# A third shared block between attention and experts, with all row scatters issued there

## The chip, the cores and the metric

The kernel runs on one core of a Trainium2 chip. The metric is device microseconds of one execution; each version is run several times and the median is given. A profiled execution leaves a page and a trace, from which the readings come. The engines are PE (TensorE matmul; PEld is its weight load), DVE (VectorE), ACT (ScalarE), POOL (GpSimd) and SP (SyncE, used for DMA issue).

## The reference

One transformer layer on x of 4 x 1024 tokens with D = 256, all in float32.

```
x = x + xattn(layernorm(x), ctx)      # 16 heads, 77 context rows, own norm with gamma, beta
x = x + ffn(layernorm(x))

ffn:  scores = softmax(xf @ Wg); weights, indices = top_k(scores, 4)      # 32 experts
      for e in experts:  y[tok] += swiglu(xf[tok], W1[e], W2[e], W3[e]) * w
      return y + swiglu(xf, Ws1, Ws2, Ws3)                                # the shared expert
swiglu(x, w1, w2, w3) = (silu(x @ w1) * (x @ w3)) @ w2
```

## The kernel before

The 4096 tokens are eight blocks of 512 (`NB`), each of four tiles of 128. The program has four stages, and in each the order of instructions on every engine is the order of the program text (`as_written`).

**Attention loop** (t = 0 to 31, L756 to L830). One tile of 128 tokens per turn, with the routing of older blocks woven in: `turn_ffn` transposes a block's normalized tokens and stores them to DRAM (`xnd`), `gate`, `chances`, `choose`, `mark`, `count` and `place` find each token's four experts and the row it takes in the expert's list. `send` then scatters rows: one indirect DMA from POOL (L674) writes 128 rows of 272 floats to `xr` in DRAM. A block has 16 of them. The loop issues four a turn from t = 11 on, which leaves the last 12 of block 5 and all of blocks 6 (`y`) and 7 (`z`).

**Between loop and experts** (L833 to L1004). The list `left` holds row scatters not yet issued, and `sends(n)` issues the next n. The routing of blocks y and z is finished here, the tables of which expert tile reads which rows are made (`tables`, a generator advanced by `next`; table "a" serves the first 64 tiles, "z" the rest), and the shared expert is computed for blocks y and z. The shared expert of a block comes in parts: `shared_in(blk, f, act)` does eight PE passes of 512 columns (L704) and the activation on ACT (L713), `shared_mid(blk, f)` multiplies on DVE into hT (L719, or L721 and L722 for block y), `shared_out(blk)` does 16 PE passes (L730) and `shared_add(blk)` two DVE additions onto the result y0 (L743). In this stage hT has one buffer and sg two; PSUM has eight banks, all under one tag.

**Experts** (L1126 to L1183). 144 tiles of 128 rows. Per tile: two transposes (L1078), copy on DVE (L1080), four matmul passes (L1086), Silu on ACT (L1094) and a product on DVE (L1095), a transpose (L1100) with copy on ACT (L1102), the second matmul (L1107), scaling on DVE (L1111), and one indirect DMA from POOL that scatters the 128 result rows to `ys` (L1112), from one of six y buffers. The steps of four tiles are interleaved. SP fetches the rows of eight tiles at a time (L1024), each with its own DMA, into one of two buffers g. Fetches for the first 64 tiles wait for the scatters of blocks 0 to 5; later ones wait for all. Every third tile up to j = 45 issues one left row scatter as well (`sends(1)`). The last 16 tiles or so stand under a `Switch` on the number of tiles; shared block 0 is computed around its entry.

**End** (L1227 to L1254). The shared blocks 1 to 5, and for each half block a load of its tokens' four results from `ys` (`gather`, 1 MB, on SP), three DVE additions (`gathered`, L1204 to L1206) and a store to `out`. `adding` says which half blocks are added during which shared block; `order` begins with blocks 6 and 7.

The names of tiles in the profile: xr rows by expert, ys results by token, ph and hT the shared hidden layer, pz its output, peh an expert's hidden layer, h its activation, xnd and sx the stored tokens for the shared expert.

Of the kernel before, what the change touches and what calls it, by code (L numbers as in the profile page):

```python
# [9 lines left out]
F32 = mybir.dt.float32  # L10
I32 = mybir.dt.int32
U32 = mybir.dt.uint32
AF = mybir.ActivationFunctionType
# [17 lines left out]
def kernel(  # L31
# [723 lines left out]
    with as_written():  # L755
        for t in range(NT):  # L756
            blk, c = t // NC, t % NC
            ffn, old = blk - 1, blk - 2
            ahead = blk + 1 < NB
            if c == 0 and blk + 2 < NB:  # L760
                xts[blk + 2] = load(blk + 2)
            if t == 0:

                nc.sync.dma_start(xr[NE * PLACES :, :], none)
                nc.sync.dma_start(
                    xr[: NE * PLACES, :].rearrange("(e q) r -> q e r", q=PLACES)[:P],
                    none.unsqueeze(1).to_broadcast([P, NE, ROW]),
                )
            if t == 18:
                nc.sync.dma_start(ws13[:, :, 0, :], Ws1.rearrange("(k p) f -> p k f", p=P))  # L770
                nc.sync.dma_start(ws13[:, :, 1, :], Ws3.rearrange("(k p) f -> p k f", p=P))
                nc.sync.dma_start(ws2, Ws2.rearrange("(k p) f -> p k f", p=P))
            if t in parts:
                load_experts(*parts[t])
            if c == 1 and ahead:
                scale_in(blk + 1)
            if c == 1 and ffn >= 0:
                measure_out(ffn, 2, 4)
            if c == 3 and ahead:
                bias_in(blk + 1)  # L780
            if c == 3:
                measure_out(blk, 0, 2)
            if c == 3 and ffn >= 0:
                measure_ffn(ffn)
            if c == 1 and old >= 0:
                gate(old)
            if c == 3 and old >= 0:
                count(old)
            sv = [scores(t, g) for g in range(2)]
            if c == 1 and old >= 0:  # L790
                turn_gate(old)
                chances(old)
            soften(t, 0, sv[0])
            if c == 1 and old >= 0:
                powers(old)
            soften(t, 1, sv[1])
            sv.append(scores(t, 2))
            if t >= 1:
                for i in range(3):
                    turn_p(t - 1, i)  # L800
            soften(t, 2, sv[2])
            if c == 0 and old >= 0:
                turn_ffn(old)
            if c == 2 and ahead:
                turn_in(blk + 1)
            if c == 0 and ahead:
                measure_in(blk + 1)
            if c == 1 and old >= 0:
                choose(old)
            if c == 2 and old >= 0:  # L810
                mark(old)
            if c == 3 and old >= 0:
                place(old)
            invert(t)
            divide(t)
            if c == 1 and ahead:
                norm_in(blk + 1)
            if c == 3 and ffn >= 0:
                norm_ffn(ffn)
            if c == 3:  # L820
                settle(blk, 0)
            elif ffn >= 0:
                settle(ffn, c + 1)
            if c >= 2 and ahead:
                keep(blk + 1, 2 * c - 4, 2 * c - 2)
            if t >= 11:
                b11, c11 = divmod(t - 11, NC)
                send(b11, c11 * TOPK, (c11 + 1) * TOPK)
            if t >= 1:
                residual(t - 1, output(t - 1))  # L830


        z, y = NB - 1, NB - 2  # L833
        assert BA == y
        msum_a = sm.tile([P, NE], F32, tag="msum_a", name="msum_a", bufs=1)
        nc.vector.tensor_copy(msum_a, cums[BA][:, 0, :])
        left = [(y - 1, i) for i in range(NK)]

        def sends(n):
            for blk, i in left[:n]:  # L840
                send(blk, i, i + 1)
            del left[:n]

        del left[:4]
        measure_out(z, 2, 3)
        settle(z, 1)
        sends(3)
        turn_ffn(y)
        for i in range(3):
            turn_p(NT - 1, i)  # L850
        settle(z, 2)
        residual(NT - 1, output(NT - 1))
        measure_out(z, 3, 4)
        gate(y)
        turn_gate(y)
        chances(y)
        powers(y)
        settle(z, 3)
        sends(2)
        measure_ffn(z)  # L860
# [94 lines left out]
    with as_written():  # L955
        for part in range(5):
            load_experts(*parts[NT + 1 + part])
        ta = tables("a", msum_a, NA)
        choose(y)
        shared_in(y, 0, AF.Tanh)  # L960
        norm_ffn(z)
        mark(y)
        sends(7)
        shared_mid(y, 0)
        next(ta)
        shared_in(y, 1, AF.Tanh)
        turn_ffn(z)
        count(y)
        gate(z)
        next(ta)  # L970
        place(y)
        assert not left
        left += [(y, i) for i in range(NK)]
        turn_gate(z)
        chances(z)
        powers(z)
        next(ta)
        shared_mid(y, 1)
        shared_out(y)
        next(ta)  # L980
        choose(z)
        shared_in(z, 0, AF.Silu)
        mark(z)
        count(z)
        msum_z = sm.tile([P, NE], F32, tag="msum_z", name="msum_z", bufs=1)
        nc.vector.tensor_copy(msum_z, cums[NB][:, 0, :])
        tz = tables("z", msum_z, NJ - NA)
        sends(5)
        shared_mid(z, 0)
        place(z)  # L990
        left += [(z, i) for i in range(NK)]
        shared_in(z, 1, AF.Silu)
        shared_add(y)
        shared_mid(z, 1)
        sends(11)
        shared_out(z)
        shared_add(z)
    late_stack.close()
# [126 lines left out]
    with as_written():  # L1125
        fetch(0)  # L1126
        for j in range(NM_ + len(steps)):
            if j % RG == 1 and j + RG - 1 <= NM_:
                fetch(j + RG - 1)
            if j in (4 * RG + 4, 5 * RG + 4, 6 * RG + 4):  # L1130
                fetch_shared(j // RG - 4, nc.sync)
            for i, step in enumerate(steps):
                jj = j - i
                if 0 <= jj < NM_:
                    made[jj, i + 1] = step(jj, made.pop((jj, i), None))
            if j % 3 == 0:
                sends(1)
            if j in (2, 5, 8, 11):
                next(tz)
            if j < NM_ and j % RG in (0, 1, 2):  # L1140
                find(j // RG * RG, j % RG)
            if j == NM_ - 2 * RG:
                more = {
                    e: nc.values_load(
                        tabs["more"],
                        engines=[e],
                        min_val=0,
                        max_val=(NJ - NM_) // RG,
                        skip_runtime_bounds_check_because="at most as many tiles as are laid out",
                    )  # L1150
                    for e in mybir.ALL_ENGINES
                }
                tc.switch_hint(more, (NJ - NM_) // RG + 1, label="more")

            if j == NM_:
                shared_in(0, 0, AF.Silu)
            if j == NM_ + 1:
                shared_mid(0, 0)
                shared_in(0, 1, AF.Silu)
            if j == NM_ + 2:  # L1160
                shared_mid(0, 1)
                fetch_shared(3, nc.scalar)
    ahead = groups[NM_ // RG][0]
    for n in tc.Switch(more, (NJ - NM_) // RG + 1, hint="more"):
        end = NM_ + n * RG
# [3 lines left out]
        with as_written():  # L1169
            for j in range(NM_, end + len(steps)):  # L1170
# [6 lines left out]
                if j < end and j % RG in (0, 1, 2):  # L1177
                    find(j // RG * RG, j % RG)
                if j == end:
                    shared_out(0)  # L1180
                if j == end + 1:
                    shared_add(0)
    bp_stack.close()  # L1183
    hs_stack.close()
    bw_stack.close()
# [31 lines left out]

    NS = NB - 2
    order = [*range(2 * NS, 2 * NB), *range(2 * NS)]
    adding = [[], [0, 1, 2, 3], [4, 5, 6], [7, 8, 9], [10, 11, 12], [13, 14, 15]]  # L1220
    with as_written():
        come = [gather(hb) for hb in order[:8]]

# [2 lines left out]
            if i + 8 < 2 * NB:  # L1226
                come.append(gather(order[i + 8]))  # L1227

        shared_in(1, 0, AF.Silu)
        shared_in(1, 1, AF.Silu)  # L1230
        shared_mid(1, 0)
        for blk in range(1, NS):
            todo = list(adding[blk])
            last = blk == NS - 1
            if blk + 3 < NS:
                fetch_shared(blk + 3, nc.scalar)
            for i in todo[:1]:
                add(i)
            shared_mid(blk, 1)
            for i in adding[blk - 1]:  # L1240
                store(order[i])
            if last:
                store(order[todo[0]])
            if not last:
                shared_in(blk + 1, 0, AF.Silu)
            shared_out(blk)
            for i in todo[1:2]:
                add(i)
            if not last:
                shared_mid(blk + 1, 0)  # L1250
                shared_in(blk + 1, 1, AF.Silu)
            for i in todo[2:]:
                add(i)
            shared_add(blk, store if last else None)  # L1254

# [54 lines left out]
```

## Time and profile before

| | us |
|---|---|
| median of 3 runs (798.32 to 802.23) | 800.97 |
| the profiled execution | 800.8 |
| its span, first to last instruction | 799.0 |
| PE busy in the span | 733.9 (92%) |
| DVE | 527.1 (66%) |
| POOL | 402.9 (50%) |
| ACT | 334.1 (42%) |

| Stage, by the trace | us from the span's start |
|---|---|
| the last attention output (L497) ends | 401.2 |
| first expert product on PE (L1086) | 449.3 |
| last row scatter (L674) | 554.7 |
| last result scatter (L1112) | 732.2 |
| first gather issued (L1196) | 735.8 |
| last addition (L743) | 794.0 |

All times are read from one execution, counted from its first instruction. A row of the timeline gives start and length in us, engine, line, operation and tiles, and in brackets the idle time of that engine before it and what ended it. "issue" is a wait for nothing that the profile shows; "remote" one that something outside the shown instructions ended. The granted clock of TensorE is 1.00 at full speed; over the span it is 0.974.

### The profile page before, as it was taken

How to read it: one execution, taken by the hardware profiler on the slowest of the kernel's cores; microseconds unless marked ns; L12 is line 12 of the kernel's file. 1: busy time of each engine (PE TensorE's matmuls, PEld its weight loads, DVE VectorE, ACT ScalarE, POOL GpSimd, SP SyncE). 2: the span in 40 equal slices, each digit the busy share in tenths (PEclk: the TensorE clock that was granted, in tenths of full speed). 3: DMA queues.
4: the chain of work that ended last, by engine and by line, in shares of the span. 5: the costliest groups of instructions: out<-in, count | busy, mean ns of one | idle time of the engine just before them, and what ended most of it. 6: DMA issues, size and time to landing. Idle time of an engine off the chain costs nothing.

```text
span 799.0 us, 12911 instructions
## 1 busy us (share of the span) xinstructions
PE 733.9 (92%) x3508; PEld 542.2 (68%) x3508; DVE 527.1 (66%) x1455; ACT 334.1 (42%) x1586; POOL 402.9 (50%) x488
## 2 busy tenths in 40 slices
PE   6999999999999999999968578879999999999796
PEld 4775767777777777776735457667888878776454
DVE  1874565778777787767665355545767666473897
ACT  0647667676666677766521112221222222221000
POOL 2003333347777777777886355555555555443000
PEclk9999999999999999999998889999999999999988
DMA  8930000404135221513175244465555545422996
GB/s 269 333 101 1 1 1 1 132 1 141 58 100 185 80 98 57 162 57 115 57 242 169 75 125 136 138 197 165 189 165 162 182 146 160 149 96 90 412 412 246
DMA packets 78867, 111.97 MB, mean 140 GB/s; under 512 B 9995, under 2 KB 63679, under 8 KB 78783
## 3 DMA queue, kind: packets, MB, share of 16 engines
q1 hardware_dynamic: 59519, 66.14, 26.7%
q0 software_dynamic: 13056, 36.72, 12.7%
q10 hardware_dynamic: 6208, 8.17, 2.9%
q8 instruction: 31, 0.51, 0.3%
q14 instruction: 53, 0.43, 0.2%
HBM read 62.36 MB, written 48.64 MB: 139 GB/s over the span
## 4 chain that ended last, share of the span: by engine, by line
PE 72%; DVE 10%; ACT 6%; issue 4%; DMA 4%; POOL 3%; DVEq 0%; ACTq 0%; SPq 0%; POOLq 0%
PE peh L1086 16%; PE po L497 14%; PE sc L430 13%; PE py L1107 7%; ACT p L446 5%; PE pgT L1078 4%; PE ph L704 3%; PE pz L730 3%; PE pp L479 2%; PE phT L1100 2%; PE pvo L262 1%; POOL xr L674 1%; PE pvo L287 1%; PE pm L262 1%; DMA gy<-ys 1%
## 5 line engine op out<-in xcount | busy, mean ns | idle before, releaser
L1112 POOL DMA_INDIRECT ys<-y,place x144 | 138.0, 959 | 130.0 <-DVE y L1111 81.2
L446 ACT ACTIVATE p<-sc,mx 128x77 f32<-128x77 f32 x512 | 159.1, 350 | 93.2 <-DVE mx L438 93.2
L1086 PE MATMUL peh<-we,gT 128*128 x576 | 155.0, 393 | 17.7 <-issue 11.4
L497 PE MATMUL po<-we,pT 128*128 128x256 f32 (+1 forms) x640 | 147.1, 383 | 4.6 <-DVE pT L484 3.3
L674 POOL DMA_INDIRECT xr<-xn,row x128 | 127.6, 997 | 35.6 <-issue 34.6
L461 POOL TENSOR_TENSOR p<-p,su 128x385 f32<-128x385 f32 (+1 forms) x96 | 91.0, 973 | 97.2 <-DVE su L456 76.3
L430 PE MATMUL sc<-we,qT 128*128 128x385 f32 (+1 forms) x384 | 138.9, 509 | 0.9 <-POOL qT L416 0.9
L497 PEld LDWEIGHTS po<-we,pT 128*128 128x128 f32 (+1 forms) x640 | 118.4, 190 | 26.7 <-DVE pT L484 5.4
L1094 ACT ACTIVATE h<-peh 128x128 f32<-128x128 f32 x144 | 40.1, 278 | 217.2 <-PE peh L1086 143.8
L1086 PEld LDWEIGHTS peh<-we,gT 128*128 128x128 f32 x576 | 101.5, 196 | 29.7 <-issue 12.8
L446 ACT ACTIVATION_READ_ACCUMULATOR p<-sc,mx 128x1 f32 x512 | 118.7, 232 | 0.0
L430 PEld LDWEIGHTS sc<-we,qT 128*128 128x128 f32 x384 | 71.1, 189 | 54.3 <-issue 27.7
L1095 DVE TENSOR_TENSOR h<-peh,h 128x128 f32<-128x128 f32 x144 | 41.8, 291 | 84.6 <-ACT h L1094 69.1
L1107 PE MATMUL py<-we,ehT 128*128 x288 | 88.3, 389 | 0.9 <-ACT ehT L1102 0.8
L1111 DVE TENSOR_SCALAR y<-py,own 128x256 f32<-128x256 f32 x144 | 69.5, 483 | 17.2 <-PE py L1107 13.1
L438 DVE TENSOR_REDUCE mx<-sc 128x5 f32<-128x385 f32 (+1 forms) x96 | 54.3, 576 | 33.8 <-PE sc L430 31.3
L1080 DVE COPY gT<-pgT 128x256 f32<-128x256 f32 x144 | 59.8, 415 | 7.4 <-PE pgT L1078 4.8
L1078 PE MATMUL pgT<-ident,g 128*128 128x128 f32 x288 | 55.9, 278 | 1.1 <-issue 0.4
L1107 PEld LDWEIGHTS py<-we,ehT 128*128 128x128 f32 x288 | 44.5, 195 | 12.6 <-ACT ehT L1102 1.7
L1078 PEld LDWEIGHTS pgT<-ident,g 128*128 128x128 f32 x288 | 40.6, 144 | 16.9 <-issue 1.6
L1100 PE MATMUL phT<-ident,h 128*128 128x128 f32 x144 | 40.2, 279 | 8.2 <-DVE h L1095 5.9
L730 PE MATMUL pz<-ws,hT 128*128 128x256 f32 x128 | 35.5, 431 | 11.8 <-DVE hT L719 6.3
(200 smaller groups left out, 927.4 us busy)
## 6 DMA issues: line engine op xcount, KB each, us to landing
g<-xr SPq DMA_DIRECT2D x144, 136.0 KB
gy<-ys SPq DMA_DIRECT2D x16, 1024.0 KB
xr<-y SPq DMA_DIRECT2D x1, 4352.0 KB
y<-in_x SPq DMA_DIRECT2D x8, 512.0 KB
out<-y ACTq DMA_DIRECT2D x16, 256.0 KB
xnd<-xnT SPq DMA_DIRECT2D x6, 512.0 KB
we<-in_W SPq DMA_DIRECT2D x8, 384.0 KB
ys<-y,place POOLq DMA_INDIRECT x144
```

What stands on the lines that cost most here:

```text
L430: nc.tensor.matmul(sc[:, : (h1 - h0) * SK], qTs[blk][:, k, o : o + P], mq[:, b, k, h0 * SK : h1 * SK], start=(k == 0), stop=(k == KC - 1),)
L446: nc.scalar.activation(probs[t][:, h, :], sv[:, h - h0, :], AF.Exp, bias=mx[:, h : h + 1], accum_out=su[:, h : h + 1],)
L461: nc.gpsimd.tensor_tensor(p[:, h0:h1, :], p[:, h0:h1, :], su[:, h0:h1].unsqueeze(2).to_broadcast([P, h1 - h0, SK]), ALU.mult,)
L497: nc.tensor.matmul(po[:, :D], pT[:n, i, :], vo[b][:n, i, :], start=(i == 0), stop=(i == KT - 1))
L674: sct = nc.gpsimd.indirect_dma_start(out=xr, out_offset=bass.IndirectOffsetOnAxis(ap=row[:, i : i + 1], axis=0), in_=xn[:, c, :], in_offse ...
L730: nc.tensor.matmul(pz[:, c * D : (c + 1) * D], hT[:, f, (2 * c2 + c) * P : (2 * c2 + c + 1) * P], ws2[:, f, :], start=(f == 0), stop=(f == ...
L1078: nc.tensor.transpose(pt[:, k * P : (k + 1) * P], g[:, j % RG, k * P : (k + 1) * P], ident)
L1080: nc.vector.tensor_copy(gT.rearrange("p k t -> p (k t)"), pt[:, :D])
L1086: nc.tensor.matmul(ph[:, : 2 * H], gT[:, k, :], we[:, ds(ev[j] * EW + k * 2 * H, 2 * H)], start=(k == 0), stop=(k == KC - 1),)
L1107: nc.tensor.matmul(py[:, :D], hT, we[:, ds(ev[j] * EW + KC * 2 * H, D)], start=True, stop=True)
L1111: nc.vector.tensor_scalar(y, py[:, :D], own[:, i, 1:2], None, ALU.mult)
L1112: sent = nc.gpsimd.indirect_dma_start(out=ys, out_offset=bass.IndirectOffsetOnAxis(ap=place_[:, i : i + 1], axis=0), in_=y, in_offset=None,)
```

## The change

Block 0's shared expert moves from the switch into the stage between loop and experts. Its tokens are loaded from `xnd` into a buffer of the attention loop (tag qb), on SP. All row scatters of blocks y and z are issued in that stage, in two runs of 12 and 20, with `place(z)` between them; the expert loop issues none. `choose(z)` stands ahead of `shared_out(y)`. Block 1 takes block 0's place in the switch. The end computes the shared blocks 2 to 5, and the 16 half blocks are spread four to a block.

```
+        sxs[0] = late.tile([P, NC, D], F32, tag="qb", name="sx_0", bufs=3)
+        sxs[0] = sxs[0].rearrange("p c d -> p (c d)").rearrange("p (k t) -> p k t", k=KC)
+        nc.sync.dma_start(sxs[0], xnd[0])
         z, y = NB - 1, NB - 2
...
         next(ta)
         shared_mid(y, 1)
+        shared_in(0, 0, AF.Silu)
+        choose(z)
         shared_out(y)
         next(ta)
-        choose(z)
-        shared_in(z, 0, AF.Silu)
         mark(z)
+        shared_mid(0, 0)
+        shared_in(0, 1, AF.Silu)
         count(z)
...
         tz = tables("z", msum_z, NJ - NA)
-        sends(5)
-        shared_mid(z, 0)
+        sends(12)
         place(z)
         left += [(z, i) for i in range(NK)]
+        shared_mid(0, 1)
+        shared_in(z, 0, AF.Silu)
+        shared_add(y)
+        shared_out(0)
+        shared_mid(z, 0)
         shared_in(z, 1, AF.Silu)
-        shared_add(y)
+        shared_add(0)
         shared_mid(z, 1)
-        sends(11)
+        sends(20)
+        assert not left
         shared_out(z)
         shared_add(z)
...
             if j in (4 * RG + 4, 5 * RG + 4, 6 * RG + 4):
-                fetch_shared(j // RG - 4, nc.sync)
+                fetch_shared(j // RG - 3, nc.sync)
...
-            if j % 3 == 0:
-                sends(1)
...
             if j == NM_:
-                shared_in(0, 0, AF.Silu)
+                shared_in(1, 0, AF.Silu)
...
-                fetch_shared(3, nc.scalar)
+                fetch_shared(4, nc.scalar)
...
-    adding = [[], [0, 1, 2, 3], [4, 5, 6], [7, 8, 9], [10, 11, 12], [13, 14, 15]]
+    adding = [[], [], [0, 1, 2, 3], [4, 5, 6, 7], [8, 9, 10, 11], [12, 13, 14, 15]]
...
-        shared_in(1, 0, AF.Silu)
-        shared_in(1, 1, AF.Silu)
-        shared_mid(1, 0)
-        for blk in range(1, NS):
+        shared_in(2, 0, AF.Silu)
+        shared_in(2, 1, AF.Silu)
+        shared_mid(2, 0)
+        for blk in range(2, NS):
...
-            for i in todo[:1]:
+            for i in todo[: 1 + last]:
                 add(i)
             shared_mid(blk, 1)
             for i in adding[blk - 1]:
                 store(order[i])
             if last:
-                store(order[todo[0]])
+                for i in todo[:2]:
+                    store(order[i])
```

The rest of block 0's calls in the switch (`shared_mid`, `shared_out`, `shared_add`) change to block 1 in the same way.

More of the change, by code (lines that the diff above doesn't have):

```diff
@@ L1155 @@
             if j == NM_:
-                shared_in(0, 0, AF.Silu)
+                shared_in(1, 0, AF.Silu)
             if j == NM_ + 1:
-                shared_mid(0, 0)
-                shared_in(0, 1, AF.Silu)
+                shared_mid(1, 0)
+                shared_in(1, 1, AF.Silu)
             if j == NM_ + 2:
-                shared_mid(0, 1)
-                fetch_shared(3, nc.scalar)
+                shared_mid(1, 1)
+                fetch_shared(4, nc.scalar)
     ahead = groups[NM_ // RG][0]
@@ L1179 @@
                 if j == end:
-                    shared_out(0)
+                    shared_out(1)
                 if j == end + 1:
-                    shared_add(0)
+                    shared_add(1)
     bp_stack.close()
@@ L1246 @@
             shared_out(blk)
-            for i in todo[1:2]:
+            for i in todo[1 + last : 2 + last]:
                 add(i)
@@ L1251 @@
                 shared_in(blk + 1, 1, AF.Silu)
-            for i in todo[2:]:
+            for i in todo[2 + last :]:
                 add(i)
```

## The prediction

> **What bounds the kernel now.** I read the busy rows by slice first, then a table of stages, then the timelines of POOL and ACT inside the worst stage, and last the chain of waits.
>
> ```profile
> POOL 2003333347777777777886355555555555443000
> PEclk9999999999999999999998889999999999999988
> ```
>
> Slices 22 to 28 (some 420 to 560 us) are the only long stretch in which the TensorE clock drops and POOL's share falls. The stage table puts sizes to it; its columns are busy us with the count for PE, PEld, DVE, ACT and POOL, then granted clock, DMA share and GB/s.
>
> ```profile
> 405.00:441.00 36.00, 26.78 (x104) 15.34 (x102) 22.68 (x86) 6.62 (x12) 25.09 (x31) 0.91 0.69 214
> 441.00:449.30 8.30, 0.07 (x2) 0.03 (x1) 1.12 (x4) 0.00 (x0) 3.86 (x5) 0.81 0.37 123
> 449.30:559.30 110.00, 93.66 (x448) 72.38 (x448) 56.99 (x189) 21.24 (x95) 57.50 (x60) 0.92 0.43 139
> 559.30:637.40 78.10, 77.34 (x427) 65.30 (x427) 55.62 (x183) 20.84 (x96) 45.49 (x48) 1.00 0.55 172
> 735.70:795.30 59.60, 50.22 (x148) 29.64 (x146) 52.30 (x67) 5.34 (x9) 0.00 (x0) 0.93 0.92 361
> ```
>
> Rows three and four are the same work. ACT's h (L1094) runs once per expert tile: tile 0 at 451.38, tile 48 at 559.30, tile 96 at 637.82. The first 48 tiles take 107.9 us, the next 48 take 78.5 (undisturbed, eight take 13.02). So 29.4 us are lost in the first 48. What differs is POOL: 60 indirect DMAs against 48. Of the 60, 15 are row scatters (L674), the last at 554.7; PE is gapless soon after.
>
> ```profile
> 482.16 0.96 POOL L674 DMA_INDIRECT xr<-xn,row  x1 [0.30 <-issue]
> 483.43 0.96 POOL L1112 DMA_INDIRECT ys<-y,place  x1 [0.30 <-issue]
> 484.69 0.96 POOL L1112 DMA_INDIRECT ys<-y,place  x1 [0.30 <-issue]
> 485.95 0.96 POOL L1112 DMA_INDIRECT ys<-y,place  x1 [0.30 <-issue]
> 487.22 0.96 POOL L674 DMA_INDIRECT xr<-xn,row  x1 [0.30 <-issue]
> 490.72 0.96 POOL L1112 DMA_INDIRECT ys<-y,place  x1 [2.54 <-DVE eq L1040]
> ```
> ```profile
> 489.45 0.28 ACT L1094 ACTIVATE h<-peh 128x128 f32<-128x128 f32 x1 [4.54 <-PE peh L1086]
> ```
> ```profile
> 572.40 0.96 POOL L1112 DMA_INDIRECT ys<-y,place  x1 [0.67 <-DVE eq L1040]
> ```
>
> An indirect DMA holds POOL 0.96 us at a pitch of 1.265. Three tiles with one row scatter need 4 x 1.265 = 5.06 us, while PE needs 3 x 1.627 = 4.88: POOL runs out of slack and goes back to back. After four or five in a row the other engines answer late: ACT waits 4.54 us for a matmul long finished and goes on 1.3 us after the chain's last scatter ends. Without rows every scatter has 0.67 us ahead of it, and no such wait is seen. The same at the start of the experts, at the end of an uncut run of row scatters (431 to 446):
>
> ```profile
> 445.12 0.96 POOL L674 DMA_INDIRECT xr<-xn,row  x1 [0.30 <-issue]
> 448.18 0.69 DVE L743 TENSOR_TENSOR y<-pz,y 128x512 f32<-128x512 f32 x1 [8.55 <-remote]
> 449.30 2.05 PE L1086 MATMUL peh<-we,gT 128*128 x4 [8.23 <-issue]
> ```
>
> I call this a freeze: it ends 2.1 us after POOL's chain (446.08 to 448.18), and the first h comes 3.2 us later.
>
> **The change, part by part.** The sum is made against the profiled execution, 800.8 us (span 799.0), 0.2 below the median 800.97.
>
> *Row scatters out of the experts.* Sixteen leave POOL's queue (one at every third tile). The first 48 tiles then look like the next 48, which have the same SP fetches, eight per 13 us: 107.9 becomes 78.5. I leave 3.4 us of it (the first eight tiles took 16.46 against 13.02; cold clock and table work at j = 2, 5, 8, 11 stay). Gain 26.0.
>
> *The same rows between loop and experts.* POOL now issues 12 rows, the three small writes of place(z), then 20 rows. From 419.6 (first row of block 6): 12 x 1.265 reaches 434.8, the writes 435.4, 20 x 1.265 reaches 460.7; before it ended at 446.1, with a hole of 5.5 us ahead of 431.18 that is filled now. Queued behind on POOL are the result scatters, which the six y buffers cover for some tiles; the freeze is not covered. SP's fetches of tiles 0 to 15 start as before once r_tab is there (429.2, now perhaps 427.5, because p_r comes after a warm shared_out) and fall into the chain. So the freeze ends at about 460.4 + 2.1 = 462.5. I let progress inside it be such that only a piece of shared_out(z) is left (1.3 us of 3.45), as before the engines still went on for 9 us into the chain: first h at 462.5 + 1.3 + 3.2 = 467, 15.6 later than 451.4. Both ends: with no freeze the work alone decides (rival A); with nearly everything still to do, rival B.
>
> *The third shared block.* Its PE cost is two shared_in and one shared_out:
>
> ```profile
> 763.75 6.87 PE ph L704 x16
> 770.62 3.45 PE pz L730 x16
> ```
>
> 10.3 us on PE, and on DVE two mids and two adds at a pitch of 0.60, 2.4 us; two sg on ACT, 0.6 each. Between loop and experts it can lie in a hole:
>
> ```profile
> 421.30 5.44 PE L730 MATMUL pz<-ws,hT 128*128 128x256 f32 x14 [5.09 <-DVE hT L722]
> ```
>
> shared_in(0,0), 3.44 us, fits in the 5.09; the matmuls behind it no longer run at half clock (5.44 for what takes 3.0). So 10.3 costs 10.3 - 5.1 - 2.4 = 2.8 on PE, hidden under POOL's chain in my main case. Other moves: choose(z) goes ahead of shared_out(y), 2.3 us of DVE in DVE's 5.98 us wait for p_r; hT has one slot, so mid(z,0) waits for shared_out(0). count(z) now stands behind shared_in(0,1), which makes row_z some 3.4 us later, about 432; POOL asks for it only at 440.3, behind the last four rows of y. If PSUM's eight banks let shared_in(0,0) start only once mid(y,1) has freed two (421.25), the hole stays and PE pays 7.9 instead of 2.8, still under the chain of POOL. The load of sx_0 is one SP issue of 0.34 (as the stores of xnT), in a queue with little to do between 323 and 401, into the buffer of qb that block 5 has left. If that cover were gone, 0.3 us. Later fetches only change numbers, and SP still issues three of them in the loop; ACT keeps its one there and loses one at the end.
>
> *Switch.* Block 1 replaces block 0: same instructions, nothing.
>
> *End.* The tail has 16 gathered adds, and DVE carries it: busy 52.3 of 54.8 us.
>
> ```profile
> 740.50:795.30 54.80, 52.30 (x67) 0.93 0.94 369
> ```
>  One block less takes 2.4 us of DVE, and 10.3 of PE, which is hidden. But DMA is also at 412 GB/s until 780, so the gain lies between 0 and 2.4, nearer to DVE's row: 2.0. The other split of adds moves nothing: the last block again ends on two adds and its own.
>
> Sum: +15.6 - 26.0 - 2.0 = -12.4; 800.8 - 12.4 = 788.
>
> **A rule weighed.** The Trainium skill, "SBUF — State Buffer", section "Who interferes with whom", says that only the port pair shared by VectorE and GpSimd contends, and that DMA never contends with a compute engine. By it POOL's longer chain would cost PE and ACT nothing: the first h comes at 446 (as in rival A), sum -5.4 - 26.0 - 2.0, 767 us. The trace speaks against it here: ACT and PE, which have no part in that pair, wait 4.54 and 8.23 us until POOL pauses. I follow the rows.
>
> **Rivals.**
> A, *mild freeze.* PE finished its old work at 441.06; plus 2.8, plus 2 for gT and peh, is a first h at 446, 5.4 earlier. POOL is then behind until 460.7 and has to catch up at 1.627 - 1.265 = 0.36 us a tile, so I allow one freeze of 8 us, the size of that at 441. -5.4 + 8 - 26.0 - 2.0: 775. For it: from 419.6 to 425.7 POOL ran back to back and DVE to PE still took 0.05 us. Against: that chain was of five, this one of 32.
>
> B, *the freeze catches the shared blocks early*, and the change is slower. Place: wakeups between PE, ACT and DVE from about 428. Left at 462.5 are shared_in(z,0), shared_out(0), shared_in(z,1), shared_out(z): 13.8; half clock in the first 6.8 us (as the granted clock was 0.5 from 446.2 to 453.0) adds 3.4; three handoffs of sg and mid, which the single hT slot puts in series, 3.9; then 3.2. First h at 486.8, +35.4 - 28.0 = +7.4: 808. It turns slower from a first h at 479.4. Against: the z rows need place(z), so an early freeze starves POOL near 440 and ends itself.
>
> C, *half of that work left*: first h at 475, +23.6 - 28.0, 796.
>
> D, *the rows were not the cause* and the first 48 tiles stay slow (first use of the weights, say): +15.6 - 2.0, 814. Against: the loss ends within two tiles of the last row.
>
> **How the numbers follow.** Main case 0.45 (788, its own range 780 to 795), A 0.25, C 0.12, B 0.12, D 0.06. A measurement of this kernel can tell about 0.5%, 4 us, from no change. Faster by more: 0.45 + 0.25 + half of C, 0.76. Within: half of C, 0.02 of B, 0.08. Slower: 0.10 of B and D, 0.16. The range, 771 to 807, takes in A down to a short freeze and half of B; D, the rest of B, and A without any freeze are left out.
>
> **What would show it.** Right: no L674 after some 462; tiles 0 to 48 in about 82 us with 0.67 ahead of each L1112; clock 1.0 from 470 on; first h near 467 with DVE or PE idle until POOL's chain ends; the stretch of DVE in the tail 2 us shorter. Wrong: h of the early octets still over 16 us (D); first h at 446 to 455 (A) or after 475 (B, C); PE's wait at 416 to 421 not filled, which would put the 10.3 us on the path.

## The result and the profile after

The changed kernel takes 795.41 us (median of four runs, 794.32 to 795.89) where the kernel before took 801.44 beside it: a ratio of 0.9937, 95% interval 0.9908 to 0.9966 (the two medians alone give 0.9925). That is 5 to 6 us faster, where 12.4 were forecast. The profiled execution took 795.5 us with a span of 793.7.

The two rows by slice that showed the trouble before read as follows in the changed kernel:

```profile
POOL 2003333346878777786887354555555555534000
PEclk9999999999999999999999688999999999999997
```

The clock, which lay at 0.8 in three slices before, now dips to 0.6 in the slice from 436 to 456 us and stays at 0.8 for two more. POOL's share in that slice is 0.3, as it was in the same slice before. The stage table has the same columns as before (busy us with the count for PE, PEld, DVE, ACT and POOL, then granted clock, DMA share, GB/s):

```profile
401.00:420.10 19.10, 15.29 (x78) 7.32 (x77) 13.72 (x57) 5.58 (x13) 15.44 (x19) 1.00 0.81 249
420.10:440.40 20.30, 8.31 (x29) 4.58 (x28) 3.67 (x20) 1.61 (x2) 15.86 (x19) 0.81 0.30 108
440.40:449.80 9.40, 4.11 (x8) 2.38 (x9) 6.10 (x17) 0.60 (x1) 0.02 (x1) 0.50 0.39 114
449.80:471.60 21.80, 17.11 (x59) 10.96 (x58) 5.86 (x11) 1.20 (x2) 15.39 (x16) 0.92 0.47 155
471.60:555.20 83.60, 79.52 (x424) 65.78 (x425) 55.57 (x186) 20.48 (x93) 42.33 (x44) 0.96 0.48 153
555.20:633.60 78.40, 78.40 (x435) 66.24 (x434) 55.43 (x181) 20.84 (x96) 45.56 (x48) 1.00 0.56 175
731.50:790.00 58.50, 43.49 (x122) 25.13 (x121) 50.17 (x64) 4.18 (x7) 0.00 (x0) 0.91 0.93 360
```

In the second row mainly POOL works (15.9 of 20.3 us, all row scatters and the small writes between them): PE does 8.3 us, DVE 3.7, ACT 1.6, all of it before 429.3, and the DMA engines are at 0.30. The first 48 tiles (fifth row) are nearly as dense as the next 48 now. With ACT's h again as the clock of the tiles, the difference between the two profiled executions is:

| stretch | before | after | difference | forecast |
|---|---|---|---|---|
| start to the first h | 451.38 | 473.53 | +22.15 | +15.6 |
| first h to the 49th | 107.92 | 83.70 | -24.22 | -26.0 |
| 49th h to the last | 165.96 | 165.68 | -0.28 | 0 |
| last h to the end | 73.75 | 70.77 | -2.98 | -2.0 |
| sum | | | -5.33 | -12.4 |

One term is far off, the first. The timeline between loop and experts shows where it went; first POOL, then the other engines (start, duration, instruction, and in brackets the idle time before it with what ended it):

```profile
420.11 1.00 POOL L674 DMA_INDIRECT xr<-xn,row  x1 [0.28 <-issue]
421.41 0.96 POOL L674 DMA_INDIRECT xr<-xn,row  x1 [0.30 <-issue]
...
439.43 0.96 POOL L674 DMA_INDIRECT xr<-xn,row  x1 [0.30 <-issue]
449.78 0.96 POOL L674 DMA_INDIRECT xr<-xn,row  x1 [9.39 <-DVE hT L719]
```
```profile
443.43 0.21 DVE L938 TENSOR_SCALAR r_tab_a<-p_r_a 1x64 int32<-1x64 f32 x1 [17.93 <-remote]
443.53 0.60 ACT L713 ACTIVATE sg<-ph 128x512 f32<-128x512 f32 x1 [20.81 <-remote]
445.04 6.78 SPq L1035 DMA_DIRECT2D g<-xr  x12
445.69 0.79 PE L638 MATMUL pf<-mask,tri 128*128 128x128 f32 x2 [16.40 <-DVE mask L626]
```

DVE's r_tab needs only p_r, a pair of matmuls that ended at 425.3. It starts 18 us later, at 443.43, 3.0 us after the end of the scatter of 439.43. ACT's sg needs a product that PE had begun at 425.60 and finished by 429.3, and starts at 443.53, at least 14 us late (the 20.81 in its row is all of ACT's idle time); PE waits for DVE. Even DVE's own results come late to DVE, by 0.98 us ahead of L606 at 425.00. This is the prediction's freeze; in the experiments it is called a stop. The chain of waits carries it, and a second one behind the z rows, as time that nothing in the profile explains:

```profile
425.50 17.95 another core or an unknown queue
457.80 15.71 another core or an unknown queue
```

The second piece is not all lost time, because PE and DVE worked in its first part: POOL had been issuing at full pitch since 452.85, and up to 463.1 both still took up each other's results within about 0.1 us. The late answers begin with gT, 2.3 us after the transposes ended (463.46), and h starts 5.9 us after the first product (L1097) ended (467.66) and 2.0 us after POOL's last row:

```profile
465.75 0.42 DVE L1091 COPY gT<-pgT 128x256 f32<-128x256 f32 x1 [1.99 <-remote]
473.53 0.28 ACT L1105 ACTIVATE h<-peh 128x128 f32<-128x128 f32 x1 [15.73 <-remote]
```

### The profile page after: what moved, and what is told of

It reads as the page before. It is cut to its first block, busy times and chain, and to the rows that moved or that the text cites. A ratio compares the mean times of both kernels' runs of the same rounds, so it can differ in the third digit from the quotient of the medians.

```text
span 793.7 us, 12911 instructions
## 1 busy us (share of the span) xinstructions
PE 726.8 (92%) x3508; PEld 540.2 (68%) x3508; DVE 526.8 (66%) x1455; ACT 334.3 (42%) x1586; POOL 403.3 (51%) x488
## 4 chain that ended last, share of the span: by engine, by line
PE 66%; DVE 12%; ACT 6%; DMA 4%; another core or an unknown queue 4%; POOL 3%; issue 3%; SPq 0%; DVEq 0%; ACTq 0%; POOLq 0%
PE peh L1097 15%; PE po L497 14%; PE sc L430 13%; PE py L1118 7%; ACT p L446 5%; PE pgT L1089 4%; PE pp L479 2%; DVE gy L1213 2%; PE phT L1111 2%; PE ph L704 2%; DMA gy<-ys 2%; DVE y L1214 1%; POOL xr L674 1%; PE pvo L262 1%
## 5 line engine op out<-in xcount | busy, mean ns | idle before, releaser
L1097 PE MATMUL peh<-we,gT 128*128 x576 | 151.9, 387 | 7.6 <-DVE gT L1091 7.1
L1097 PEld LDWEIGHTS peh<-we,gT 128*128 128x128 f32 x576 | 99.9, 193 | 17.2 <-DVE gT L1091 8.4
L1118 PE MATMUL py<-we,ehT 128*128 x288 | 86.6, 383 | 0.0
L1122 DVE TENSOR_SCALAR y<-py,own 128x256 f32<-128x256 f32 x144 | 69.6, 483 | 11.3 <-PE py L1118 10.3
L479 PEld LDWEIGHTS pp<-ident,p 128*128 128x128 f32 x320 | 36.1, 138 | 11.4 <-issue 5.5
```

What stands on the lines that cost most here:

```text
L1097: nc.tensor.matmul(ph[:, : 2 * H], gT[:, k, :], we[:, ds(ev[j] * EW + k * 2 * H, 2 * H)], start=(k == 0), stop=(k == KC - 1),)
L1118: nc.tensor.matmul(py[:, :D], hT, we[:, ds(ev[j] * EW + KC * 2 * H, D)], start=True, stop=True)
L1122: nc.vector.tensor_scalar(y, py[:, :D], own[:, i, 1:2], None, ALU.mult)
```

## The experiments

The times depend on the chip that a run lands on. On three of the chips that these runs saw (numbers 2, 4 and 8) the kernel before takes 799 to 800 us, as in the runs above; on three others (3, 13 and 14) it takes 760. I call them the 800 chips and the 760 chips; every ratio is against runs of before on the same chip. The columns "first h" and "48 tiles" are read from one profiled execution each.

Theory: an unbroken run of POOL's row scatters holds the other engines' wakeups back; this costs the 22 us, and the rows among the result scatters cost the 26 us. Rivals: the third block's own work makes the first h late; or the number and the bytes of the rows count, not how they are spaced.

**Halves of the change, and more or fewer rows ahead of the experts (chip 14).** The rows alone, on the kernel before:

```
-        sends(11)
+        sends(27)
...
-            if j % 3 == 0:
-                sends(1)
```

> Only the scatter part of the change on the kernel before: runs of 5 and 27 rows between loop and experts, none in the experts; no third block there. Theory T (POOL issuing indirect DMAs back to back, more than about five, withholds the wakeups of the other engines until it pauses): the run of 27 goes from about 431 to 466, the first h (L1094) comes at 466 to 471 instead of 451, the first 48 expert tiles take 82 to 86 us instead of 107.9; 792 to 798 us. Theory V (the late first h of the changed kernel is the third block's own work and its handoffs): first h at 450 to 455, 776 to 782 us. Theory D (the slow first 48 tiles have another cause than the rows): they still take over 100 us, and the time is above 801.

The third block alone, on the changed kernel (rows back in the experts):

```
-        sends(12)
+        sends(5)
...
-        sends(20)
-        assert not left
+        sends(11)
...
+            if j % 3 == 0:
+                sends(1)
```

> Only the third block and the shorter end; the rows as in the kernel before: 5, then 11, and 16 in the experts. Theory T: no stop at 425 to 443, POOL has its hole there; first h at 452 to 457, one wait of 5 to 9 us at the end of the run of 11; first 48 tiles 105 to 109 us; 797 to 802 us. Theory V: first h at 468 to 474 as in the changed kernel, 815 to 820 us. Theory D: first 48 tiles as in T.

All rows ahead, but split 5 and 27:

```
-        sends(12)
+        sends(5)
...
-        sends(20)
+        sends(27)
```

> The changed kernel with its rows in runs of 5 and 27 instead of 12 and 20. Theory T: the stop of 16 us at 429 to 446 is gone, since POOL stands idle until idx of block z is there; r_tab comes at about 426 and the fetches of rows at 428; the second run lasts from about 427 to 463 and stops the engines from about 438; first h at 464 to 470, 785 to 792 us. Theory V: first h stays at 472 to 475, 794 to 797 us.

A pause behind every row from block 6 on: a power of one column (`pad`, set to 1 once, ahead of it), which keeps POOL busy for 0.57 us and feeds nothing.

```
                 send(blk, i, i + 1)
+                if blk >= BA:
+                    nc.gpsimd.tensor_tensor(pad, pad, neg_half[:, 0:1], ALU.pow)
```

> The changed kernel with one small POOL operation (a power of 128 x 1, about 0.6 us) behind each of the 32 rows of blocks 6 and 7, so that rows come at 1.9 us instead of 1.265; bytes and number of rows are the same. Theory T, if a pause in the DMAs is enough though POOL is busy: no wait over 3 us on PE between 425 and 446, first h at 446 to 455; the rows last to about 482, the result scatters queue behind them, and tile 48 comes at 545 to 560; 785 to 800 us. If only an idle POOL ends a stop: the stop lasts as long as the longer runs, first h at 485 to 500, 808 to 825 us. Theory V: first h at 472 to 475.

| kernel, chip 14 (before 759.79) | us | ratio (interval) | first h | 48 tiles |
|---|---|---|---|---|
| rows alone | 772.49 | 1.0163 (1.0134 to 1.0192) | 442.11 | 94.24 |
| third block alone | 761.36 | 1.0021 (1.0011 to 1.0032) | 443.95 | 80.42 |
| 5 and 27 | 766.92 | 1.0095 (1.0078 to 1.0112) | 445.30 | 83.80 |
| paused | 787.70 | 1.0360 (1.0343 to 1.0377) | 445.58 | 106.39 |

My four expectations, written for a chip like the first, missed: before takes 40 us less on this chip, and there is no stop here to take away. So before and after had to be seen again on such a chip.

**Before and after on a 760 chip (chip 13).** No edit.

> The kernel before, once more with a profile, since the four experiments so far ran on a chip on which it takes 759.8 us instead of 801. Theory T as a property of the chip (one on which POOL's back-to-back indirect DMAs withhold wakeups, another on which they don't): where it takes some 760 us, no wait of PE over 3 us between 401 and 560, first h at 440 to 443, the first 48 tiles 79 to 82 us; where it takes some 800 us, the page of the first profile again. If the rows slow the experts on every chip (the rival), the first 48 tiles take over 100 us on this one too.

> The changed kernel on the same chip. On a chip without withheld wakeups: PE pays 2 to 4 us for the third block, first h at 443 to 446, POOL's rows last until 461, the result scatters queue behind them and the six y buffers run out: PE waits 4 to 8 us once in the first 16 tiles; the end is 2 to 3 us shorter; 761 to 766 us, slower than before by 0.2 to 0.8%. On a chip with them: as measured, 795 us, 0.6% faster than before.

Before took 761.34 (median of its runs there 760.58), after 767.36, ratio 1.0102 (1.0078 to 1.0127), a little above the 761 to 766 us expected: the change makes the kernel slower on this chip. The changed kernel on it, at the two instructions that tell most:

```profile
423.59 0.21 DVE L938 TENSOR_SCALAR r_tab_a<-p_r_a 1x64 int32<-1x64 f32 x1 [1.32 <-PE p_r_a L934]
463.04 0.48 DVE L1122 TENSOR_SCALAR y<-py,own 128x256 f32<-128x256 f32 x1 [3.36 <-DMA ys<-y,place]
```

r_tab is answered after 1.32 us, though POOL issues the same chain at the same pitch (422.15, 423.42, 424.69 and so on). So the chain alone is not enough; chip and chain together make the stop. What it costs here is something else: the last row starts at 459.3, the first result scatter at 460.55, 15.8 us behind the first h (5.4 us in before), and the six y buffers cover some 12 us of it (15.8 less the 3.36 of the row above). DVE has to wait for a free y, and PE behind it. The first h comes 2.1 us later than in before, the 48 tiles take 3.3 us more, and the end 1.4 us less; that is 3.9 us between the two profiled executions. The other three runs of after are 1.5 to 4.2 us longer than the profiled one, at a lower granted clock (0.980 to 0.986 against 0.989); no trace of them was kept. "Rows alone" and "paused" are the same wait made longer: 22.5 and 34.5 us behind, PE idle 9.46 and 21.68. And before has nothing to win: with its rows in the experts, the first 48 tiles take 80.43. (One wait of PE is over the 3 us that I had expected at most, 4.78 us for hT at 420.21: the hole that the third block fills.)

**Fewer rows ahead, and the split, on an 800 chip (chip 2, before 800.36).** Six rows go back into the experts, one every eight tiles:

```
-        sends(20)
-        assert not left
+        sends(14)
...
+            if j % RG == 0 and 0 < j < 7 * RG:
+                sends(1)
```

> The changed kernel with the last six rows of block z left to the experts, one behind every eighth tile (j = 8 to 48). On a chip where before takes some 760 us: POOL's run ends 7.6 us sooner, the first result scatter comes 8 us behind the first h instead of 15.8, which six y buffers cover (they covered about 12), so the wait of PE at 461 to 464 goes and the first 48 tiles take 80 to 81 us instead of 83.7; 761 to 764 us against 767.4 of the changed kernel. If the loss there has another cause than the queue on POOL, 83 to 84 us and no change. On a chip where before takes some 800 us: first h 5 to 8 us sooner than 473.5, early tiles slower by as much as chains of four behind each row cost; 790 to 796 us.

> The changed kernel with its rows in runs of 5 and 27, a second look. On a chip where before takes some 760 us: as in the first look, first h at 445, first 48 tiles 83.8 us, 765 to 768 us. On a chip where before takes some 800 us, theory T: the stop of 16 us at 429 to 446 is gone and the engines stop in the second run instead; first h at 464 to 470, 785 to 792 us; if the stop stays at 429 to 446, it is not the uninterrupted run of scatters that starts it.

Six rows late: 796.27, ratio 0.9949 (0.9926 to 0.9972), first h 465.16, 48 tiles 87.63. On chip 8 it took 797.16 (0.996, 0.9941 to 0.9979). What the shorter chain wins at the first h goes back in tiles, and a few answers stay late behind the last row (553.82) too, so the prediction's "without rows no such wait is seen" is not quite true. The split of 5 and 27, a single run, gave 796.32 with the first h at 473.75: the same stop as in after, 18.18 us for r_tab. By the last words of the expectation this speaks against the theory, but the run was not interrupted: I had thought that POOL would stand idle behind the five; it doesn't, because choose(z) has moved ahead and the next idx is there when POOL asks (rows at 424.76 and 426.26, with only the small writes between them).

**choose(z) back behind shared_out(y), on a 760 chip (chip 3, before 759.78).** With 5 and 27 rows, and on the changed kernel:

```
-        choose(z)
         shared_out(y)
         next(ta)
+        choose(z)
```

> The changed kernel with choose(z) back behind shared_out(y) and the tables, where the kernel before has it, and the rows in runs of 5 and 27. On a chip where before takes some 800 us, theory T: POOL now stands idle until idx comes, so the tables are read at about 427 as before and the stop at 428 to 445 is gone or moved into the run of 27 rows, where it ends when POOL does, near 466; first h at 468 to 478, 790 to 799 us. If the stop stays at 428 to 445, a hole in POOL's run does not prevent it. On a chip where before takes some 760 us: 764 to 769 us.

768.38, ratio 1.0104 (1.0041 to 1.0168), where 5 and 27 had 1.0095: no stop occurs here, and its place makes no difference that can be told. On this chip the paused kernel again gave 1.0352 (1.032 to 1.0384), the third block alone 1.0028 (1.002 to 1.0036). This order was not run on an 800 chip.

**The pause on an 800 chip (chip 8, before 799.77).**

> The changed kernel with a POOL operation of about 0.6 us behind each of the 32 rows. On a chip where before takes some 800 us, theory T, if rows at 1.9 us are far enough apart: no wait of PE over 3 us between 425 and 446, first h at 445 to 450, then about 22 us of waiting for y buffers as on the other chips; 788 to 794 us. If any load of row scatters stops the engines, pauses or not: the stop stays, first h after 480, over 805 us. On a chip where before takes some 760 us: 786 to 790 us.

A single run: 788.55. The stop at 425 is gone; the same rows follow each other at 1.83 us in place of 1.27:

```profile
422.73 1.04 POOL L674 DMA_INDIRECT xr<-xn,row  x1 [0.18 <-issue]
423.80 0.57 POOL L850 TENSOR_TENSOR pad<-pad,neg_half 128x1 f32<-128x1 f32 x1
424.56 1.04 POOL L674 DMA_INDIRECT xr<-xn,row  x1 [0.20 <-issue]
```
```profile
424.33 0.21 DVE L943 TENSOR_SCALAR r_tab_a<-p_r_a 1x64 int32<-1x64 f32 x1 [1.31 <-PE p_r_a L939]
481.96 2.07 PE L1102 MATMUL peh<-we,gT 128*128 x4 [19.84 <-DVE own L1076]
```

The first line below POOL's is the instruction that waited 17.93 us in after. The first h is at 445.47, 28 us sooner than in after. On the same chip the kernel with six rows late, which has no pauses, shows the stop: 18.67 us for r_tab. Number and bytes of the rows are unchanged, so the rival falls: spacing decides. (The pause also lowers the rate of the rows by 30%; whether the gap or the rate matters is not told apart.) The third block's own work is unchanged too, so that rival falls with it. Most of the gain is spent on the second line: the last row starts at 476.3, the y buffers run out, and PE waits 19.84 us.

**Where the pauses go, and the third block alone, on an 800 chip (chip 4, before 800.04).** First the third block alone, as above:

> The third block is computed and the rows stay in the experts, as in the two runs of this kernel before (1.002 and 1.003 of before, on chips where before takes 760). On such a chip: 762, the first h near 444, the first 48 tiles 80.4. On a chip where before takes 800, both theories agree that choose(z) ahead lets GpSimd issue its five and eleven rows without a pause, so a stop should come near 425 as in after: the first h near 470 (the theory of unbroken scatters) with the 48 tiles still near 107 (rows among result scatters) and 815 to 822 in all. If what matters is that rows lie in the experts and not their run before them, the first h is near 446 and the time near 798.

The same with the pause behind every row, so that the experts' rows have it too:

```
                 send(blk, i, i + 1)
+                if blk >= BA:
+                    nc.gpsimd.tensor_tensor(pad, pad, neg_half[:, 0:1], ALU.pow)
```

> As the kernel with the third block alone, but a power of one column (0.58 us, busy) follows every row on GpSimd, from the loop's end into the experts. Theory (unbroken scatters hold the other engines back): on a chip where before takes 800 no stop at 425 to 445, the first h near 445; in the experts a pause comes after each four scatters, four times 1.27 and 0.58 being 5.6 us for three tiles where 5.0 are to be had, so the first 48 tiles take about 90 in place of 108: 445 + 90 + 166 + 71 + 2 = 774. On a chip where before takes 760 it only costs: 90 for 80.4, so 770. Rival (the number or the bytes of the rows among the results matter, not the lack of pauses): the first h 445, but the 48 tiles stay near 108: 792 on the first kind of chip.

The changed kernel with the pause behind one row in three (against the paused kernel):

```
-                if blk >= BA:
+                if blk >= BA and i % 3 == 2:
```

> After with the power behind one row in three in place of none, and of each row as in the paused kernel. Theory: chains of three are too short to hold the others back for long, and the rows end at about 470 in place of 477 (ten powers of 0.58 in place of 27 and more), so TensorE's wait for a free result buffer falls from 19.8 to about 12: near 778 on a chip where before takes 800, where paused took 788.5 and after 796. On a chip where before takes 760: about 777, where after takes 767.5 and paused 787. Rival (only a pause behind every row prevents the stop): the first h stays near 470 on the first kind of chip and the time is 800 or above.

The third block alone, with the same edit to its pauses:

> The third block with the rows in the experts, and the power behind one row in three: five pauses in the run ahead of the experts, and one in each nine tiles in them. Theory: no stop at 425 to 445, the first h near 445, but in the experts chains of ten or eleven scatters remain and the first 48 tiles take 100 to 108: 785 to 792 on a chip where before takes 800. On a chip where before takes 760: 764, one power of 0.58 in nine tiles of 15 us being 3 us over the 48 tiles where GpSimd is full. Rival (any few pauses do): the 48 tiles take near 84 on both kinds of chip, and the time is 767 on both.

| kernel, chip 4 | us | ratio (interval) | first h | 48 tiles |
|---|---|---|---|---|
| third block alone | 807.64 | 1.0095 (1.0062 to 1.0129) | 460.94 | 105.70 |
| its every row paused | 784.88 | 0.9806 (0.9777 to 0.9835) | 445.52 | 98.89 |
| after, one row in three paused | 782.12 | 0.9778 (0.9743 to 0.9814) | 455.85 | 86.75 |
| third block, one row in three paused | 797.62 | 0.9979 (0.9966 to 0.9993) | 452.36 | 105.25 |

In the third block alone the stop is there as well, though all its rows but 16 stay in the experts:

```profile
438.44 0.21 DVE L938 TENSOR_SCALAR r_tab_a<-p_r_a 1x64 int32<-1x64 f32 x1 [14.62 <-remote]
```

Its chain runs to 438.79 + 0.96 without a gap, since idx no longer comes late. DVE is let go 1.3 us before the chain ends, ACT (sg at 442.71) 3.0 us after it: the end of the chain is not a sharp bound. So half of the change alone makes an 800 chip slower, and the rows bring it back and more. My sizes missed: the first h came 9 us sooner than the 470 of the first theory, and the 48 tiles of the fully paused one took 98.9, not 90 (784.88 us, not 774): four scatters in a row still bring late answers there (ACT waits 4.67 us for an h in the second group of eight, which took 21.41 us). With a pause behind one row in three the third block alone keeps its 105 us of tiles, as its first theory had it; a few pauses do not do there. Its stop, which was to be gone, was only shortened (5.95 us for r_tab, first h at 452.36 and not near 445), so it took 797.62 us and not 785 to 792. In the changed kernel one pause in three is a compromise between stop and delay:

```profile
431.70 0.21 DVE L943 TENSOR_SCALAR r_tab_a<-p_r_a 1x64 int32<-1x64 f32 x1 [7.66 <-remote]
433.97 0.79 PE L638 MATMUL pf<-mask,tri 128*128 128x128 f32 x2 [5.12 <-DVE mask L626]
```

The stop is not gone (7.66 us for r_tab), against my theory that chains of three are too short for one, and 782.12 us is 4 more than forecast. But it lets go while POOL is still issuing, the last row starts at 465.0, and the first result scatter comes 10.5 us behind the first h, so no engine waits for a y buffer. This version was run once more, on chip 2 (before 798.94):

> The changed kernel with the power behind one row in three, once more, to see it on a chip where before takes 760. There no stop is to be taken away, and the powers only put the last row off (first result scatter about 20 us behind the first h in place of 15.8), so about 775 to 778, slower than before by 2%, where after takes 767.5. On a chip where before takes 800: again near 782.

It took 782.41, ratio 0.9781 (0.9747 to 0.9815), first h 454.69, 48 tiles 90.03. So on the two 800 chips where it ran it takes 2.2% less than before, where after, on another run of such a chip, had 0.6%; it did not land on a 760 chip, where the full pause costs 3.5%.

## Where the prediction was right, and where it failed

*The rows out of the experts, -26.0: right, -24.2.* The groups of eight tiles from the third on take 13.02 us but for one of 13.26, as foreseen, with the expected 0.67 ahead of most scatters:

```profile
487.06 0.96 POOL L1123 DMA_INDIRECT ys<-y,place  x1 [0.66 <-DVE y L1122]
```

The first two take 15.48 and 15.90. Case D is out. The 760 chips add what the profile of before could not tell: the rows as such cost nothing there (80.4 us with them in the experts), so POOL's lack of slack alone does not make the loss; the 24 us go with the late answers beside it.

*The third block's cover: right in kind.* shared_in(0,0) closed the hole at 416 to 421, and the product behind it ran at full clock:

```profile
421.82 3.29 PE L730 MATMUL pz<-ws,hT 128*128 128x256 f32 x14 [0.88 <-DVE hT L722]
```

My sum for its price on PE was wrong: it took off the whole hole of 5.1 us, though what goes into the hole is 3.44 long, so it should have been 10.3 - 3.4 - 2.4 = 4.5 and not 2.8. Where nothing stops, the first h comes 43.51 us after the last attention output in the third block alone (chips 14 and 3) and 41.32 us after it in before (chip 13): 2.2 us. PE's smaller waits, up to 0.94 us each, are filled as well. So the 2.8 came near by luck.

*The end, -2.0: right, -3.0 measured.* In the last stretch DVE is busy 50.17 us against 52.30. The third block alone on a 760 chip has 70.75 us behind the last h against 72.63, and the other executions with this end lie between 70.2 and 72.9, so the missing microsecond is within their spread.

*The first h, +15.6: wrong, +22.15.* This step failed, and with 6.5 us it is nearly all of the 7 us by which the sum was off. I let the engines go on for 9 us into the chain, as before, with r_tab at about 427.5 and SP's fetches behind it, so that only a piece of shared_out(z) would be left at the end of one freeze. The stop began by 425.5, five scatters into block 6's rows, before any fetch of SP (the first is at 445.04), and caught r_tab, count(z) and nearly all of the shared blocks. That is rival B's mechanism, and B's "against" came true as well: POOL starved for the z rows at 440.4, the stop ended 3.0 us later, the blocks were computed in 443 to 458 (the first of it at half clock), and the z rows made a second stop, which let go of h at 473.5. So the time fell near case C's 796 by luck, not for C's reason (one freeze with half of the work left).

The reading behind the mistake: before's chain at 419.61 was followed by 4.5 us of waiting for idx, and I took the quiet beside it as a sign that the other engines get on well next to a chain. r_tab was answered inside that wait:

```profile
427.23 0.21 DVE L934 TENSOR_SCALAR r_tab_a<-p_r_a 1x64 int32<-1x64 f32 x1 [5.98 <-PE p_r_a L930]
430.11 0.72 POOL L650 COPY xn<-idx 128x16 f32<-128x16 f32 x1 [4.46 <-DVE idx L612]
```

I counted the hole as time that the change fills (5.5 us of POOL) and not as the pause that it takes away. I did list choose(z) as moved ahead, and priced it on DVE only; by the third block alone, where the stop is 14.62 us, and by the split of 5 and 27, where it is the same as in after, its price lies on POOL's chain. That the hole protected them, and that choose(z) alone takes it away, is argued from these traces, not shown, since its old place with the third block was not run on an 800 chip.

*The rule weighed.* The Trainium skill, "SBUF — State Buffer", section "Who interferes with whom", has it that DMA never contends with a compute engine; by it I had 767. On the 760 chips r_tab's 1.32 us beside the chain fits that sum. On the 800 chips 17.93 us do not, but the page speaks of SBUF's ports, and no run here shows that ports make the answers late: the rule is not refuted, it does not cover this wait. Even where it fits, the change does not gain, because the y buffers become the limit.

*Not in any case:* that result scatters queued behind the rows outlast six y buffers. I named the queue and took the buffers to cover it "for some tiles". On an 800 chip the stop hides this (the first h comes after the last row); take the stop away and it is the next bound.

Open: why some chips hold the wakeups back and others do not. POOL's pitch (1.265 us) and everything up to the loop's end are alike on both. Open too is what starts a stop: in after's first run the late answers begin by the fifth row of block 6, in its second only behind the ninth scatter at the same pitch. And the profiler's recording is an untested rival: every run here has a span and a clock from it, so none shows the times without it, and what it recorded differs with the kind of chip. The traces of the 800 chips hold 4155 to 4681 updates of semaphores by DMAs, those of the 760 chips 8161 to 8191, and only the latter give landing times for row scatters (2.4 to 2.5 us in the median). So "remote" in a row of an 800 chip can also mean a record that is missing; the late starts themselves do not hang on it.

## What to carry to other kernels

A gap in an engine's queue can be what lets the others work: before you fill one, ask what runs in it, and price a long run of back-to-back indirect DMAs by the wakeups that it may hold back, not by its own length alone. Where work is moved ahead of a queue, count the buffers of what then stands behind it: six buffers of 1.63 us a tile cover a delay of some 10 to 12 us and no more. And a gain of under 2% from scheduling around such stops should be measured on more than one chip, since here the same change makes the kernel 0.6% faster on one and 1.0% slower on another.

## What the runs showed of the hardware that was not expected

- The same program takes 799 to 800 us on some chips and 760 on others. In before, 36 of the 40 us lie in two places: the first h (451.4 against 442.7) and the first 48 tiles (107.9 against 80.4).
- On the 800 chips, PE's finished work is not taken up by DVE and ACT for up to 18 us (r_tab in after) while POOL issues indirect DMAs at its full pitch, and for up to some 3 us more; in that stop the DMA engines are at 0.30, and no fetch runs. A run at full pitch does not do this all along: in after's second run the answers were in time for ten microseconds.
- A busy instruction of 0.57 us on POOL behind each row scatter is enough to prevent it in the run ahead of the experts; behind each third it cuts the wait from 17.9 to 7.7 us.
